# GpSimd scales all weights, ScalarE takes a small copy from VectorE, and one late layer 3 is planned shorter

## The chip, the cores and the metric

The kernel runs on one core of a Trainium2 chip. The core has five engines with a queue of instructions each, worked off in order: TensorE (PE, with its weight loads as PEld), VectorE (DVE), ScalarE (ACT), GpSimd (POOL) and SyncE (SP, which here only issues DMAs). They wait for each other through semaphores. The metric is the time of one execution on the device in microseconds (us), here the median of three.

## The reference

The input is x of shape (16, 64, 64, 256): 16 samples of 4096 tokens with 256 channels. Four layers follow each other, each of the form "x plus something computed from the group-normalized x" (`_gn`: 32 groups of 8 channels, mean and variance over a sample's tokens and a group's channels).

```python
def encode(x, embeddings):                       # layer 0
    dis = sum(xf*xf, -1) + sum(embeddings**2, 0) - 2.0 * xf @ embeddings
    return argmin(dis, -1)                       # 1024 codes
x = x + take(embeddings.T, encode(_gn(x)), axis=0)

# layer 1, rows of the 64x64 image attend within themselves
f, g, h = n @ Wf + bf, n @ Wg + bg, n @ Wh + bh  # n = _gn(x)
x = x + einsum('bhij,bhjo->bhio', sigmoid(einsum('bhik,bhjk->bhij', f, g)), h)

# layer 2, rank one attention over 4096 x 4096
x0, x1, x2 = n @ w1 + b1, n @ w2 + b2, n @ w3 + b3
sm = softmax(x0[:, :, None] * x1[:, None, :], axis=1)
x = x + sigmoid(einsum('bn,bnm->bm', x2, sm)) * n

# layer 3, linear attention with 4 heads of 32
q, k, v = split(n @ w_qkv, 3)
q = softmax(q, over the 32 channels of a head) * 32 ** -0.5
k = softmax(k, over the 4096 tokens)
out = einsum('bhde,bhdn->bhen', einsum('bhdn,bhen->bhde', k, v), q) @ w_out + b_out
x = x + layernorm(out) * gamma + beta
```

## The kernel before

**Samples in a pipeline.** Each sample goes through generators: `stats0` (statistics of x), `stage1` (layer 0, the search among 1024 codes), `layer1`, `rows2` and `stage2` (layer 2: its three rows, then its exponentials), `gate2` (layer 2's gate, and statistics for layer 3) and `stage3` (layer 3). Several samples are under way at once, each in another stage. A sample's activations go to DRAM between stages, channel-major in chunks of 512 tokens, eight chunks a sample.

**The plan.** At the end of `tile_net_kernel` (lines 938 to 974) each generator gets a start and a length in units of one search, by hand: the search of sample b starts at b and lasts 1.0; later stages follow with lags, and a stage kind never overlaps itself. A heap then steps all generators in the order of these planned times. The length says only how a generator's steps are spread among those of the others. `LEN3` (line 38) holds the length of layer 3 for the last samples, by the number of samples left (0 is the last); all others have 1.0:

```python
LEN3 = {0: 0.4, 1: 0.33, 2: 0.37}
task("layer3", end + LAG4, LEN3.get(left, 1.0), stage3(b), 160)
```

By this, layer 3 of sample 12 (the thirteenth) is planned from 15.83 to 16.83, that of sample 13 from 16.83 to 17.20, of 14 from 17.20 to 17.53, of 15 from 17.62 to 18.02. Beside sample 12's run layer 1 of sample 15 (16.06 to 16.41), its rows (16.44 to 16.54), the exponentials of sample 14 (15.93 to 16.93) and the gate of sample 13 (15.99 to 16.79).

The steps are recorded through the Tile layer, whose scheduler makes each engine's final order from this order, with what stands under `tc.high_priority(offset=URGENT)` pulled ahead, and places all semaphores. Chip and trace know only the final order of each queue.

**From statistics to weights.** `gn_finish` (lines 276 to 299) turns statistics into `scale`, `nmean` and `nbias` of 128 partitions x 2: TensorE averages over groups, ScalarE adds epsilon (line 293), GpSimd raises to the power -0.5 (line 296) and multiplies for `nbias` (line 298). The normalization isn't applied to the activations of layers 1 to 3; it is put into their weights: `scaled` (lines 301 to 308) multiplies each of two halves of a weight by that half's column of `scale`, in place, on the engine that is given:
- `layer1`, lines 459 and 460: `wfg_n` (128x64 a half) on ScalarE, `wh_n` (128x256) on VectorE. TensorE then uses them at line 464 (a bias), 163 (the row `h_row`, in `put_row`), 482 and 493 (the chunks).
- `rows2`, lines 573 to 577: `wrow_n`, 12 columns a half, on ScalarE. TensorE follows at lines 579 and 593.
- `stage3`, lines 728 and 729: `wk_n` (128x128) on ScalarE, `wqv_n` (128x256) on VectorE. TensorE follows at lines 163, 767 and 786.

Of each buffer there is one; the raw weights are loaded into it from DRAM anew for each sample by SP.

**The search.** For each chunk `norm` makes the normalized tokens and their squares on ScalarE, sums the squares on TensorE (line 357), copies the sums out of PSUM on ScalarE (`xrow`, line 362), and transposes them on TensorE into another bank (line 364). `norm_rows` (lines 366 to 369) copies four columns of that bank to `nx2` on VectorE. Per tile of 128 tokens ScalarE writes code norms plus `nx2` (line 398), TensorE multiplies (403), VectorE adds and takes the maximum (409) and finds its index (414), and GpSimd gathers the code row with an indirect DMA that adds to the tokens (415).

**The exponentials.** Each of the 64 passes of a sample takes 2048 elements per partition: ScalarE's exponential with its sum (line 645), then VectorE's product with a second SBUF tile and its sum (line 648). In layer 3 GpSimd subtracts a maximum (line 808), multiplies by a reciprocal (760) and takes a power (874).

Of the kernel before, what the change touches and what calls it, by code (L numbers as in the profile page):

```python
# [12 lines left out]
AF = mybir.ActivationFunctionType  # L13
ALU = mybir.AluOpType
AX = mybir.AxisListType

P = 128
# [17 lines left out]
LAG2 = 0.17  # L35
LAG3, LENG = 0.06, 0.8
LAG4 = 0.04
LEN3 = {0: 0.4, 1: 0.33, 2: 0.37}
FILL = ((0.05, 0.95, 2), (1.0, 1.27, 3), (1.4, 1.58, 2))
EARLY = sum(n for _, _, n in FILL)  # L40

# [2 lines left out]
def kernel(  # L44
# [7 lines left out]
    nc = tc.nc  # L52
# [17 lines left out]
    def bank(name):  # L70
        return ps_m.tile([P, 512], F32, tag="pm", name=name)
# [60 lines left out]
    def busy(t, n):  # L132

        for _ in range(n):
            nc.tensor.matmul(
                t[:, :512], lhsT=ones3, rhs=ones3.unsqueeze(1).to_broadcast([P, 4, P]), start=True, stop=True,
                skip_group_check=True,
            )
# [6 lines left out]
    def put_row(dst, v, weight, tag, plus=None, idle=0):  # L145

        v3 = small.tile([P, NK, PARTS], F32, tag="v3", name=f"v3_{tag}")
        nc.scalar.copy(v3, v.unsqueeze(2).to_broadcast([P, NK, PARTS]))
        pb = bank(f"prow_{tag}")
        busy(pb, idle)  # L150
        row = pb[:PARTS, :C]
        weight(row, v3, plus)

        for n in range(PARTS - 1):
            top = small.tile([PARTS, C], BF16, tag="ptop", name=f"top_{tag}_{n}", bufs=1)
            nc.scalar.copy(top, row)
            nc.tensor.matmul(row, lhsT=below[:, n, :], rhs=top, start=False, stop=True, skip_group_check=True)
        nc.scalar.copy(dst[0:PARTS, :], row)

    def by_weight(w):  # L160
        def make(out, v3, plus):
            for k in range(NK):
                nc.tensor.matmul(
                    out, lhsT=v3[:, k, :], rhs=w[:, k, :], start=(k == 0), stop=(plus is None and k == NK - 1),
                    skip_group_check=True,
                )
            for k in range(NK if plus is not None else 0):
                nc.tensor.matmul(
                    out[:, k * P : (k + 1) * P], lhsT=plus[:, k, :], rhs=ident, start=False, stop=(k == NK - 1),
                    skip_group_check=True,  # L170
                )
        return make
# [61 lines left out]
    wrow_raw = const.tile([P, NK, 4], F32, name="wrow_raw")  # L234
# [14 lines left out]
    for n in range(2):  # L249
        t = const.tile([P, CH, 2, ROW], F32, name=f"blk_{n}")  # L250
# [4 lines left out]
    for n in range(4):  # L255
        t = const.tile([P, 8], F32, name=f"m8_{n}")
# [44 lines left out]
    def scaled(t, scale, engine):  # L301

        for k in range(NK):
            v = t[:, k]
            if engine is nc.scalar:
                nc.scalar.activation(v, v, AF.Copy, scale=scale[:, k : k + 1])
            else:
                engine.tensor_scalar(v, v, scale[:, k : k + 1], None, ALU.mult)
# [20 lines left out]
    def stage1(b):  # L329
        tag = f"s1_{b}"  # L330
        scale, _, nbias = norm0.pop(b)
        src = xT[b].rearrange("(k p) n -> p k n", p=P)
        tok = x[b].rearrange("(t p) c -> p t c", p=P)
        xt, xc, xn, nx2, pxt = {}, {}, {}, {}, {}
# [31 lines left out]
        def norm_rows(ch):  # L366
            px = pxt.pop(ch)
            nx2[ch] = small.tile([P, CH], F32, tag="x2", name=f"nx2_{tag}_{ch}")
            nc.vector.tensor_copy(nx2[ch], px[:, :P].rearrange("p (t n) -> p t n", n=32)[:, :, 0])  # L369

        st1 = stats_tile(1, f"st1_{tag}")
        x1_d[b] = []
# [15 lines left out]
        load(1)  # L388
        norm(0)
        norm_rows(0)  # L390
        tokens(0)
        yield 4
# [48 lines left out]
    def layer1(b):  # L441
        tag = f"l1_{b}"
        scale, nmean, _ = norm1.pop(b)
        x1 = x1_d.pop(b)
        wfg_n = wts.tile([P, NK, 2 * CK], F32, tag="wfg_n", name=f"wfg_{tag}")
        load_wfg(wfg_n)
        wh_n = wts.tile([P, NK, C], F32, tag="wh_n", name=f"wh_{tag}")
# [8 lines left out]
        load(1)  # L456
        with tc.high_priority(offset=URGENT):

            scaled(wfg_n, scale, nc.scalar)
            scaled(wh_n, scale, nc.vector)  # L460
            pb = bank(f"pb_{tag}")
            for n in range(4):
                for k in range(NK):
                    nc.tensor.matmul(
                        pb[n * CK : (n + 1) * CK, 0:1], lhsT=wfg_n[:, k, (n // 2) * CK : (n // 2 + 1) * CK],
                        rhs=nmean[:, k : k + 1], start=(k == 0), stop=(k == NK - 1),
                    )
            bfg_n = small.tile([P, 1], F32, tag="bfg_n", name=f"bfg_{tag}")
            nc.scalar.activation(bfg_n, pb[:, 0:1], AF.Identity, bias=bfg)
            put_row(h_row, nmean, by_weight(wh_n), f"h_{tag}", plus=bh3)  # L470
# [96 lines left out]
    def rows2(b):  # L567
        tag = f"r2_{b}"
        scale, nmean, _ = norm2[b]
        with tc.high_priority(offset=URGENT):  # L570
            pb = bank(f"pbr_{tag}")
            busy(pb, 3)
            for k in range(NK):
                nc.scalar.activation(
                    wrow_n[:, k, :].rearrange("p (j n) -> p j n", n=32)[:, :, 0:3],
                    wrow_raw[:, k : k + 1, 0:3].to_broadcast([P, 4, 3]), AF.Copy, scale=scale[:, k : k + 1],
                )
            for k in range(NK):
                nc.tensor.matmul(
                    pb[:, 0:1], lhsT=wrow_n[:, k, :], rhs=nmean[:, k : k + 1], start=(k == 0), stop=(k == NK - 1)  # L580
                )
            brow_n = small.tile([P, 1], F32, tag="brow_n", name=f"brow_{tag}")
            nc.scalar.activation(brow_n, pb[:, 0:1], AF.Identity, bias=brow)
        x01 = small.tile([P, NT, 2], F32, tag="x01", name=f"x01_{tag}", bufs=2)
        rd = dram.tile([3, 2, 4, CW], F32, tag="rows", name=f"rows_{tag}", bufs=3)
        for h in range(2):
            pr = bank(f"pr_{tag}_{h}")
            for j in range(4):
                xt = xb.tile([P, NK, CW], F32, tag="xb", name=f"xr_{tag}_{h}_{j}")
                nc.sync.dma_start(out=xt, in_=x2_d[b][4 * h + j])  # L590
                part = slice(32 * j, 32 * j + 32)
                for k in range(NK):
                    nc.tensor.matmul(
                        pr[part, :], lhsT=wrow_n[:, k, part], rhs=xt[:, k, :], start=(k == 0), stop=(k == NK - 1)
                    )
            rows = s1p.tile([P, CW], F32, tag="t4", name=f"rows_{tag}_{h}", bufs=3)
            nc.scalar.activation(rows, pr, AF.Identity, bias=brow_n)
            for n in range(3):
                nc.scalar.dma_start(out=rd[n, h], in_=rows[n : n + 97 : 32, :])
            pt = bank(f"prt_{tag}_{h}")  # L600
            for t in range(CH):
                nc.tensor.transpose(pt[:, t * P : (t + 1) * P], rows[:, t * P : (t + 1) * P], ident)
            nc.vector.tensor_copy(
                x01[:, 16 * h : 16 * h + 16, :].rearrange("p (j t) n -> p j t n", t=CH),
                pt.rearrange("p (t j n) -> p j t n", j=4, n=32)[:, :, :, 0:2],
            )
            yield 4
        rows_d[b] = x01, rd, [spread_rows(rd, b, 0)]

    def spread_rows(rd, b, h):  # L610

        x0b = s2p.tile([P, TOK // 2], F32, tag="x0b", name=f"x0b_{b}_{h}", bufs=2)
        x2b = s2p.tile([P, TOK // 2], F32, tag="x2b", name=f"x2b_{b}_{h}", bufs=2)
        for dst, n in ((x0b, 0), (x2b, 2)):
            nc.sync.dma_start(
                out=dst, in_=rd[n : n + 1, h, :, :].rearrange("o j n -> o (j n)").to_broadcast([P, TOK // 2])
            )
        return x0b, x2b
# [98 lines left out]
    def stage3(b):  # L717
# [3 lines left out]
        scale, nmean, xm_ = norm3.pop(b)  # L721
        wk_n = wts.tile([P, NK, P], F32, tag="wk_n", name=f"wk_{tag}")
        nc.sync.dma_start(out=wk_n, in_=w_src[:, :, 1, :])
        wqv_n = wts.tile([P, NK, 2 * P], F32, tag="wqv_n", name=f"wqv_{tag}")
        nc.sync.dma_start(out=wqv_n[:, :, 0:P], in_=w_src[:, :, 0, :])
        nc.sync.dma_start(out=wqv_n[:, :, P:], in_=w_src[:, :, 2, :])
        with tc.high_priority(offset=URGENT):
            scaled(wk_n, scale, nc.scalar)
            scaled(wqv_n, scale, nc.vector)
            put_row(qv_row, nmean, by_weight(wqv_n), f"qv_{tag}")  # L730
        yield 4

# [29 lines left out]
        for ch in range(NCHUNK):  # L762
# [18 lines left out]
            for pr in range(CH // 2):  # L781
                pqv = bank(f"pqv_{tag}_{ch}_{pr}").rearrange("p (j n) -> p j n", j=2)
                for j in range(2):
                    t = 2 * pr + j
# [111 lines left out]
        for ch in range(NCHUNK):  # L896
# [4 lines left out]
            for pr in range(2):  # L901
                if pr == 1 and ch + 1 < NCHUNK:
                    deviate(ch + 1)
                px = bank(f"pxo_{tag}_{ch}_{pr}").rearrange("p (j c) -> p j c", c=C)
                for j in range(2):
                    t = 2 * pr + j
# [5 lines left out]
                for j in range(2):  # L912
                    t = 2 * pr + j
# [38 lines left out]
    for b in range(nb):  # L952
# [9 lines left out]
        else:  # L962
            end = task("exps", end + LAG2, 0.65, stage2(b, NCHUNK), 200)
        task("layer3", end + LAG4, LEN3.get(left, 1.0), stage3(b), 160)
    for _ in stats0(0):
# [3 lines left out]
    while queue:  # L969
        now, n = heapq.heappop(queue)  # L970
# [40 lines left out]
```

## Time and profile before

| | us |
|---|---|
| median of 3 executions | 5653.41 |
| lowest, highest | 5650.06, 5654.34 |
| the profiled execution | 5630.88 |
| its span, first to last instruction | 5629.1 |
| mean granted TensorE clock | 0.964 |

The costliest groups of instructions of that execution:

| line, engine | what | count | busy us | mean ns |
|---|---|---|---|---|
| 648 DVE | exponentials times x2, sum | 1024 | 2388.3 | 2340 |
| 645 ACT | exponentials, sum | 1024 | 2138.5 | 2089 |
| 403 PE | search, tokens by codes | 4096 | 1971.2 | 615 |
| 415 POOL | gather of code rows | 512 | 1140.5 | 2228 |
| 414, 409 DVE | index of the maximum, maximum | 512 each | 622.7, 620.1 | 1217, 1213 |
| 398 ACT | code norms plus token norm | 512 | 583.3 | 1145 |
| 808, 760 POOL | layer 3, subtract, multiply | 128 each | 249.7, 198.0 | 1951, 1547 |

How to read it: "busy" is the time an engine works on such instructions. A row of a group also has the idle time of the engine just before these instructions and what ended it, so it names what an engine waited for; the view of waits lists the same by pair. A window of the trace gives busy times for a stretch alone. Matmuls are pipelined and their ends modelled, so a busy TensorE need not be at its peak.

### The profile page before, as it was taken

To read this page: it belongs to the slowest core of one execution; us is meant where nothing else is said; L and a number is where in the kernel's file an instruction comes from. 1 tells how busy PE (TensorE), PEld (TensorE's weight loads), DVE (VectorE), ACT (ScalarE), POOL (GpSimd) and SP (SyncE) were. 2 spreads that over 40 slices of the span, in tenths; PEclk is the share of its full clock that TensorE was granted. 3 is DMA by queue.
4 is the path that set the end of the run, shared out by engine and by line. 5 is a ranking of instruction groups with operands and counts; after the bars stand their busy time and mean duration, and the time that the engine had idled before them with its cause. 6 is when DMAs were issued, how large, how long until landed. Compare 5 with 4: busy or idle time off the path is not lost. (4 is left out here: it accounts for less than half of the span.)

```text
span 5629.1 us, 76169 instructions
## 1 busy us (share of the span) xinstructions
PE 5138.9 (91%) x26927; PEld 3174.3 (56%) x26927; DVE 5068.5 (90%) x7186; ACT 4560.2 (81%) x6642; POOL 1832.7 (33%) x1076
## 2 busy tenths in 40 slices
PE   7977989989999999999999999999999999997788
PEld 3533446545656556565655656565565656665566
DVE  7579789899999999999999999999999999988982
ACT  4468589788879888887988888798888979888873
POOL 2223223323333333433333343333334334321231
PEclk9988999999999999999999999999999999998889
DMA  8552744755665757566575756757575675745643
GB/s 253 173 184 73 227 132 123 226 166 174 192 214 150 235 156 228 184 204 221 164 251 152 230 175 207 228 155 247 154 226 183 204 226 152 231 152 193 203 158 121
DMA packets 521366, 1059.26 MB, mean 188 GB/s; under 512 B 52505, under 2 KB 266393, under 8 KB 512793
## 3 DMA queue, kind: packets, MB, share of 16 engines
q1 hardware_dynamic: 406288, 885.11, 46.9%
q0 software_dynamic: 73728, 67.14, 8.5%
q10 hardware_dynamic: 40968, 102.13, 4.7%
q8 instruction: 214, 3.51, 0.3%
q14 instruction: 168, 1.37, 0.1%
HBM read 751.18 MB, written 303.04 MB: 187 GB/s over the span
## 5 line engine op out<-in xcount | busy, mean ns | idle before, releaser
L648 DVE CUSTOM_DVE_ANT_0 ex_s<-ex_s,x2b 128x2048 f32<-128x2048 f32 x1024 | 2388.3, 2340 | 55.7 <-ACT ex_s L645 54.2
L645 ACT ACTIVATE ex_s<-x0b,nmax_s,x_r 128x2048 f32<-128x2048 f32 x1024 | 2138.5, 2089 | 40.3 <-DVE num_s L648 28.8
L403 PE MATMUL pd_s<-e,xn_s 128*128 128x512 f32 x4096 | 1971.2, 615 | 54.0 <-DVE m L409 41.8
L415 POOL DMA_INDIRECT xc_s<-in_emb_rows,i_s x512 | 1140.5, 2228 | 1778.4 <-DVE i_s L414 1274.6
L403 PEld LDWEIGHTS pd_s<-e,xn_s 128*128 128x128 f32 x4096 | 747.3, 196 | 786.9 <-issue 666.4
L409 DVE CUSTOM_DVE_ANT_0 nn_s<-pd_s,nn_s 128x1024 f32<-128x1024 f32 x512 | 620.1, 1213 | 114.4 <-PE pd_s L403 72.3
L414 DVE FIND_INDEX8 i_s<-m,nn_s 128x8 uint32<-128x1024 f32 x512 | 622.7, 1217 | 0.0
L398 ACT ACTIVATE nn_s<-ne,nx_s 128x1024 f32<-128x1024 f32 x512 | 583.3, 1145 | 40.7 <-DVE nx_s L369 24.8
L493 PE MATMUL ph_l<-wh_l,xt_l 128*128 128x256 f32 x2048 | 522.2, 392 | 33.8 <-DVE m L409 27.5
L786 PE MATMUL pqv_s<-wqv_s,xk_s 128*128 128x256 f32 x2048 | 489.3, 381 | 0.0
L493 PEld LDWEIGHTS ph_l<-wh_l,xt_l 128*128 128x128 f32 x2048 | 383.2, 194 | 144.9 <-issue 72.7
L786 PEld LDWEIGHTS pqv_s<-wqv_s,xk_s 128*128 128x128 f32 x2048 | 389.4, 191 | 120.7 <-issue 60.8
L808 POOL TENSOR_TENSOR qv_s<-qv_s,qm_s 128x512 f32<-128x512 f32 x128 | 249.7, 1951 | 580.6 <-DVE qm_s L807 316.0
L874 POOL TENSOR_TENSOR lrs_s<-lrs_s,mhalf 128x4 f32<-128x4 f32 x128 | 172.3, 1346 | 662.7 <-ACT lrs_s L873 655.3
L760 POOL TENSOR_TENSOR qv_s<-qv_s,qd_s 128x512 f32<-128x512 f32 x128 | 198.0, 1547 | 378.2 <-DVE qd_s L759 249.5
L378 PE MATMUL pt_s<-ident,xc_s 128*128 128x128 f32 x1024 | 163.0, 288 | 127.6 <-DMA xc_s<-in_emb_rows,i_s 102.3
L533 PE MATMUL po_l<-blk,h_l 128*128 128x128 f32 x2048 | 272.5, 282 | 3.2 <-DVE m L409 3.2
L533 PEld LDWEIGHTS po_l<-blk,h_l 128*128 128x128 f32 x2048 | 251.2, 194 | 36.8 <-issue 19.9
L914 PE MATMUL pxo_s<-wctx_s,qo_s 128*128 128x256 f32 x1024 | 267.8, 385 | 0.0
L767 PE MATMUL pk_s<-xk_s,wk_s 128*128 128x512 f32 x512 | 252.5, 616 | 1.4 <-DMA xk_s<-x_g 1.4
L378 PEld LDWEIGHTS pt_s<-ident,xc_s 128*128 128x128 f32 x1024 | 123.2, 147 | 191.7 <-DMA xc_s<-in_emb_rows,i_s 120.4
L919 ACT COPY y_s<-pxo_s 128x512 f32<-128x512 f32 x256 | 147.6, 580 | 103.2 <-PE pxo_s L918 102.4
(206 smaller groups left out, 7372.6 us busy)
## 6 DMA issues: line engine op xcount, KB each, us to landing
xs_s<-in_xT SPq DMA_DIRECT2D x128, 512.0 KB
xt_s<-in_xT SPq DMA_DIRECT2D x128, 512.0 KB
xc_s<-in_x SPq DMA_DIRECT2D x128, 512.0 KB
x_s<-xt_s ACTq DMA_DIRECT2D x128, 512.0 KB
xt_l<-x_s SPq DMA_DIRECT2D x128, 512.0 KB
x_l<-xt_l SPq DMA_DIRECT2D x128, 512.0 KB
xr_r<-x_l SPq DMA_DIRECT2D x128, 512.0 KB
xg_g<-x_l SPq DMA_DIRECT2D x128, 512.0 KB
```

Of the source, the lines that this page charges most:

```text
L378: nc.tensor.transpose(pt[:, t * P : (t + 1) * P], xc[ch][:, t, k * P : (k + 1) * P], ident)
L398: nc.scalar.activation(nn, ne2, AF.Identity, bias=nx2[ch][:, t : t + 1])
L403: nc.tensor.matmul(pd[:, cols], lhsT=xn[ch][:, k, t * P : (t + 1) * P], rhs=e2[:, k, cols], start=(k == 0), stop=(k == NK - 1),)
L409: nc.vector.tensor_tensor_reduce(out=nn, in0=pd, in1=nn, scale=1.0, scalar=-3.0e38, op0=ALU.add, op1=ALU.max, accum_out=m8[:, 0:1],)
L414: nc.vector.max_index(i8, m8, nn)
L415: nc.gpsimd.indirect_dma_start(out=xc[ch][:, t, :], out_offset=None, in_=emb_rows, in_offset=bass.IndirectOffsetOnAxis(ap=i8[:, 0:1], axis=0),
L493: nc.tensor.matmul(ph[:, t, :], lhsT=X[:, k, t * P : (t + 1) * P], rhs=wh_n[:, k, :], start=(t % 2 == 0 and k == 0), stop=False, skip_grou ...
L533: nc.tensor.matmul(po[:, m : m + P], lhsT=h[:, t, k * P : (k + 1) * P], rhs=at[:, t, :, :].rearrange("p r i -> p (r i)"), start=True, stop ...
L645: nc.scalar.activation(ex, x0b, AF.Exp, bias=nmax[:, T : T + 1], scale=x01[:, T, 1:2], accum_out=den[:, h, T : T + 1])
L648: nc.vector.tensor_tensor_reduce(out=ex, in0=ex, in1=x2b, scale=1.0, scalar=0.0, op0=ALU.mult, op1=ALU.add, accum_out=num[:, h, T : T + 1],)
L786: nc.tensor.matmul(pqv[:, j, :], lhsT=xt[:, k, t * P : (t + 1) * P], rhs=wqv_n[:, k, :], start=(j == 0 and k == 0), stop=False, skip_group ...
L914: nc.tensor.matmul(px[:, j, :], lhsT=qT[:, t * P : (t + 1) * P], rhs=wctx[:, 1, :], start=False, stop=False, skip_group_check=True,)
```

## The change

Three edits. All five weights are now scaled on GpSimd, two instructions each. VectorE's copy of the token norms becomes one of ScalarE. Layer 3 of sample 12 (three samples left) gets the length 0.7, so that it is planned from 15.83 to 16.53; the starts and lengths of all other stages stay as they were.

```diff
-LEN3 = {0: 0.4, 1: 0.33, 2: 0.37}
+LEN3 = {0: 0.4, 1: 0.33, 2: 0.37, 3: 0.7}
...
-            nc.vector.tensor_copy(nx2[ch], px[:, :P].rearrange("p (t n) -> p t n", n=32)[:, :, 0])
+            nc.scalar.copy(nx2[ch], px[:, :P].rearrange("p (t n) -> p t n", n=32)[:, :, 0])
...
-            scaled(wfg_n, scale, nc.scalar)
-            scaled(wh_n, scale, nc.vector)
+            scaled(wfg_n, scale, nc.gpsimd)
+            scaled(wh_n, scale, nc.gpsimd)
...
-                nc.scalar.activation(
+                nc.gpsimd.tensor_scalar(
                     wrow_n[:, k, :].rearrange("p (j n) -> p j n", n=32)[:, :, 0:3],
-                    wrow_raw[:, k : k + 1, 0:3].to_broadcast([P, 4, 3]), AF.Copy, scale=scale[:, k : k + 1],
+                    wrow_raw[:, k : k + 1, 0:3].to_broadcast([P, 4, 3]), scale[:, k : k + 1], None, ALU.mult,
                 )
...
-            scaled(wk_n, scale, nc.scalar)
-            scaled(wqv_n, scale, nc.vector)
+            scaled(wk_n, scale, nc.gpsimd)
+            scaled(wqv_n, scale, nc.gpsimd)
```

## The prediction

> **What bounds the kernel now.** I read the engine totals first, then the chain of waits, then busy time by stage, then DVE's waits inside the steady stage, and last the rows of the edited instructions. Totals and chain:
>
> ```profile
> PE 5138.9 (91%) x26927; PEld 3174.3 (56%) x26927; DVE 5068.5 (90%) x7186; ACT 4560.2 (81%) x6642; POOL 1832.7 (33%) x1076
> ...
> PE 5%; ACT 3%; DVE 2%; DMA 1%; issue 0%; POOL 0%; ACTq 0%; SPq 0%; POOLq 0%
> ```
>
> The chain's shares add up to about 12%: it reaches back only to 4958 us, where the last search ends, so it tells of the tail alone. For the rest I cut the span by stage. GpSimd's line 629 comes once a sample: at 1309 us for sample 3, at 4924 for sample 14, and between them every 322 to 334 us. These are eleven steady periods of about 329 us (columns: window, length, busy us and count of PE, PEld, DVE, ACT, POOL, then clock, DMA share, GB/s):
>
> ```profile
> 0.00:700.00 700.00, 574.90 (x2614) 300.20 (x2614) 540.02 (x832) 412.37 (x573) 187.10 (x138) 0.91 0.60 181
> ...
> 1309.00:4924.00 3615.00, 3431.22 (x18456) 2136.80 (x18455) 3437.54 (x4838) 3115.41 (x4542) 1295.65 (x720) 0.99 0.63 198
> 4924.00:5200.00 276.00, 231.20 (x1328) 160.70 (x1327) 244.94 (x321) 233.81 (x352) 56.55 (x39) 0.91 0.52 174
> 5200.00:5490.00 290.00, 231.30 (x1105) 166.83 (x1103) 251.54 (x367) 228.27 (x352) 76.17 (x49) 0.88 0.54 179
> ```
>
> In the steady stage DVE is 95.1% busy, PE 94.9%, ACT 86%, POOL 36%: two engines are full together, and neither alone bounds. DVE idles 177 us there (3615 less 3437.54); its waits in that window say on what:
>
> ```profile
> DVE ex_s L648 <- ACT ex_s L645: 38.3, 37, 2.7
> DVE wh_l L308 <- POOL gn_s_n L296: 29.0, 11, 2.6
> DVE nkm_s L770 <- PE pk_s L767: 26.3, 18, 3.4
> ...
> DVE wqv_s L308 <- POOL gn_s_n L296: 10.8, 11, 1.7
> ```
>
> The second and fourth are the edited lines: 22 times DVE reaches a weight before GpSimd has raised the scale to its power, and holds its queue.
>
> **DVE's relief.** The edited rows over the whole run, DVE's and the ones that leave ACT:
>
> ```profile
> L306 ACT ACTIVATE wk_s<-wk_s,gn_s_n 128x128 f32<-128x128 f32 x32 | 11.0, 391 | 4.3 <-POOL gn_s_n L296 4.3
> L308 DVE TENSOR_SCALAR wqv_s<-wqv_s,gn_s_n 128x256 f32<-128x256 f32 x32 | 10.4, 364 | 16.5 <-POOL gn_s_n L296 16.5
> L308 DVE TENSOR_SCALAR wh_l<-wh_l,gn_s_n 128x256 f32<-128x256 f32 x32 | 10.4, 363 | 34.0 <-POOL gn_s_n L296 34.0
> L306 ACT ACTIVATE wfg_l<-wfg_l,gn_s_n 128x64 f32<-128x64 f32 x32 | 9.4, 340 | 27.0 <-POOL gn_s_n L296 27.0
> L574 ACT ACTIVATE wrow_n<-wrow_raw,gn_s_n 128x12 f32<-128x12 f32 x32 | 8.1, 296 | 19.8 <-POOL gn_s_n L296 19.6
> L369 DVE COPY nx_s<-pxt_s 128x4 f32<-128x4 f32 x128 | 19.4, 151 | 23.3 <-PE pxt_s L364 23.3
> ```
>
> In eleven periods DVE loses 44 scalings x 0.325 us (10.4/32) = 14.3, 88 norm copies x 0.151 = 13.3, and waits of 29.0 + 10.8 = 39.8: together 67 us, 6.1 a period. The copies' own 23.3 us of waiting lies almost wholly before 700 us, where DVE isn't full; I count none of it.
>
> **ACT.** It loses 11.0 + 9.4 + 8.1 = 28.5 us of scaling and 27.0 + 4.3 + 19.6 = 50.9 of waiting. It gains 128 copies; bounds are 0.19 us (line 148's 128x6 copy) and 0.26 (line 362's 128x128 copy out of PSUM), so 24 to 33 us. Its busy time stays. Could the copy wait? In the steady stage the transpose at line 364 ends 0.38 to 1.81 us after ACT's copy at line 362. In the built order 107 of the 128 new copies have a pass of line 645 (2.09 + 0.19 us) or 398 (1.15) in between, so I cost the wait at nothing. Were that cover gone it would be 88 x 0.81 us (the mean) = 71 us on ACT, which idles 500 us there. Line 398, which waited 24.8 us for DVE's copy, now follows on the same engine.
>
> **GpSimd.** No tensor-by-scalar operation of POOL is in the trace. Nearest rows (least, median, greatest ns):
>
> ```profile
> L298 POOL TENSOR_TENSOR gn_nb_n<-gn_nm_n,gn_s_n x48: 186/188/1841, 193.2 to 5501.9; 128x2 f32<-128x2 f32 x48
> L760 POOL TENSOR_TENSOR qv_s<-qv_s,qd_s x128: 1042/1290/3195, 859.3 to 5575.6; 128x512 f32<-128x512 f32 x128
> L808 POOL TENSOR_TENSOR qv_s<-qv_s,qm_s x128: 1038/1654/3142, 844.5 to 5572.0; 128x512 f32<-128x512 f32 x128
> ```
>
> Between 186 ns for 2 elements and 1038 for 512 lie 1.67 ns an element. My estimates: 0.20 us for wrow (12), 0.29 for wfg (64), 0.40 for wk (128), 0.61 for wh and wqv (256); above, 1.65 each (line 808's median), below, 0.19. Ten a sample take 4.2 us; POOL idles 210 us a period.
>
> All now follow line 298 (0.19 us) in one queue. wh is ready 0.19 + 0.58 + 1.22 = 2.0 us after the power, against 0.69 now; wqv 0.19 + 0.80 + 1.22 = 2.2 against 0.69. Who waits? From the end of a scaling to PE's first use the steady stage has at least 1.4 us for wfg, 4.8 for wh, 20 for wk and wqv: nothing. In samples 0 to 2 the slack of wh is 0.12 to 0.17, so PE starts 1.2 us late three times: 3.5. Sample 15's wqv has 0.27 and sample 13's 0.85: 1.3 + 0.7. wrow has none (PE starts the moment it ends): 0.19 + 0.40 against 0.53 now, 0.1 x 15 = 1.5. Sum +7; at 1.65 us an operation some +75, at 0.19 each +1. Behind them on POOL stand the gathers of line 415 and lines 808, 760, 874; ACT waits for 808 (51.4 us in 22 waits in the steady stage), so up to 2 us at one of those now and then.
>
> The row that speaks against the change: of the 1024 passes of line 648, the 750 that meet no GpSimd tensor operation average 2.28 us; 79 that meet one of line 808, 2.43; 55 with line 760, 2.88; 17 with both, 3.28; 84 with the power of line 874, 2.28. So a 1.04 us GpSimd operation costs DVE 0.15 to 0.60 us, a tiny one nothing. Ten of 0.42 us on average: 0.6 to 2.4 us a period; I take 1.0, so 11 of the 67 go back and 56 stay.
> The Trainium skill (SBUF — State Buffer, "Who interferes with whom") goes further: a VectorE instruction with two SBUF inputs, as line 648 is, and a GpSimd instruction that reads SBUF lock each other out, the later one for the whole of the earlier. By that, an estimate, 42% (2388/5629) of 4.2 us, 1.8 a period, goes back, and the forecast would be 4 us later.
>
> **Layer 3 of sample 12.** It starts at planned time 15.83 and is spread to 16.53, not 16.83; layer 3 of sample 13 keeps 16.83. Its fetches (line 764, 898, 823), stores and POOL steps move with it. In DVE's order its last step stands after pass 935 of line 648 instead of 948, the first maximum of sample 13 after 945 instead of 956; from 972 on both orders agree within two passes, so the last 139 us are untouched. From 4924 to 5490 us DVE idles 70 us, which bounds any gain; 18.8 of it lies in 5066 to 5207, where the step moves. Sample 15's rows fall 2 to 4 passes (4.2 us each) later, with over 60 us left until its first pass at 5197. I take -6; bounds -20 and +15.
>
> **The sum.** PE and DVE tie, so I let half of 56 come through: -28, +7, -6 = -27. The profiled execution has a span of 5629.1 us, 5630.9 with what lies around it; the median shown is 22.5 higher, and I carry the difference over: 5653.4 - 27 = 5626.
>
> **Rivals.**
> - DVE is the true bound and all 56 come through: -56 + 7 - 6, 5598. For: DVE's waits for PE are some 58 us of the 177. Against: PE idles only 184 us.
> - PE takes over at once: +7 - 6, 5654. For: PE's 94.9%. Against: PE itself waits for DVE's line 409 (24.4 + 16.5 us) there.
> - Slower: the scalings collide with line 648. All ten a period meet a pass and lengthen it by 1.0 us (the row that meets two): 10 - 6.1 = 3.9 lost a period, 43, half of it 22 with the +1: 5676. It decides from 0.61 us an operation, line 760's row. For: line 648 fills 42% of the span. Against: most weight operations are far smaller, and the power costs passes nothing.
> - The tail turns: sample 15's rows come over 60 us late, or the denser layer 3 stalls the passes: -28 + 7 + 40, 5672. Against: its order hardly moves.
>
> **How the numbers follow.** Half relief 0.46, full relief 0.22, PE takes over 0.12, collision 0.13, tail 0.07. A median of this kernel can be told from no change at about 0.2%, 11 us: 5642 to 5665. Half relief (own range 5605 to 5646) is faster in nine cases of ten: faster 0.41 + 0.22 + some 0.04 from the third = 0.67; same 0.05 + 0.07 = 0.12; slower 0.21. The range runs from full relief with the tail's -20 (5584, some 5 lower for relief before 1309 us) to just short of the collision: 5580 to 5672.
>
> **What would show it.** Right: the period at line 629 falls from 329 us to about 326; DVE has no waits for POOL's scale; line 648's mean stays under 2.40 us (2.34 now); PE's idle time in the steady stage shrinks below 184 us. Wrong: line 308 on POOL takes over 1 us each, or line 648 passes 2.45; PE waits for POOL at line 163 or 464 in the steady stage; the period stays while DVE's idle time grows; or the stretch after 4924 us, 705 now, changes by over 15.

## The result, and the profile after

The changed kernel takes 5691.03 us (median of 6 runs, 5683.00 to 5704.59), the kernel before on the same chip 5653.07 (6 runs, 5636.73 to 5659.93): a ratio of 1.0077, 95% interval [1.0062, 1.0091]. The change makes the kernel slower by some 38 us of median; 5626 with a range of 5580 to 5672 had been predicted. The sign was wrong, and the time lies outside the range.

The profiled execution of the changed kernel has a span of 5691.2 us. Its totals, and the group of line 648:

```profile
PE 5175.6 (91%) x26927; PEld 3187.5 (56%) x26927; DVE 5023.9 (88%) x6994; ACT 4549.4 (80%) x6674; POOL 2033.8 (36%) x1236
...
L648 DVE CUSTOM_DVE_ANT_0 ex_s<-ex_s,x2b 128x2048 f32<-128x2048 f32 x1024 | 2361.4, 2314 | 89.1 <-ACT ex_s L645 88.8
```

VectorE did get its relief: 44.6 us less busy time (5068.5 before), and the passes of line 648 became no longer (2314 ns, before 2340). VectorE loses it again as waiting: it idles 667 us of the span, 561 before. TensorE's busy time is 36.7 us longer for as many matmuls (5138.9 before), at a granted clock of 0.958 against 0.964, so these two executions differ in the clock too. The six runs of the changed kernel had 0.957 to 0.960, and 29 runs of the kernel before on another chip 0.958 to 0.964. Whether PE's waits lower the clock isn't shown.

The same steady window as before (length; busy us and count of PE, PEld, DVE, ACT, POOL; clock, DMA share, GB/s):

```profile
1309.00:4924.00 3615.00, 3430.99 (x18303) 2131.99 (x18302) 3365.05 (x4663) 3082.75 (x4527) 1413.19 (x815) 0.98 0.63 195
```

PE is busy as before (3431), but has done 153 fewer matmuls in it, and DVE idles 250 us where it idled 177. Not all of that is the change's: in the profiled execution of s_len below, whose queues differ from those of the kernel before only from 4915 us on (but for a swap of two PE instructions), the window holds 100 fewer matmuls, and DVE idles 200 us. The runs below decide on the causes; the views show where to look. The view of waits of the whole run (waiting engine, tile and line, what ended the wait; us in total, times, longest) names the places:

```profile
DVE nn_s L409 <- PE pd_s L403: 148.0, 86, 11.4
...
DVE ex_s L648 <- ACT ex_s L645: 88.8, 78, 7.0
...
ACT brow_r L583 <- PE pbr_r L579: 51.1, 15, 4.8
...
PE pbr_r L579 <- POOL wrow_n L574: 37.1, 23, 3.0
```

The same view of the kernel before, where ScalarE scales `wrow_n`, has

```profile
PE pbr_r L579 <- ACT wrow_n L574: 16.1, 10, 1.7
...
ACT brow_r L583 <- PE pbr_r L579: 8.8, 12, 2.8
```

and 72.3 and 54.2 us for the first two pairs. VectorE no longer waits for the scale, but for PE and ACT, and these stand around lines 579 and 583, behind GpSimd's `wrow_n`. DVE's waits for the scale (29.0 + 10.8 us before) are gone, as planned.

The new operations, one row for each weight (count: ns least/median/greatest, first and last start):

```profile
L308 POOL TENSOR_SCALAR wfg_l<-wfg_l,gn_s_n x32: 432/449/2572, 197.5 to 5036.1; 128x64 f32<-128x64 f32 x32
L308 POOL TENSOR_SCALAR wh_l<-wh_l,gn_s_n x32: 912/917/5096, 198.3 to 5041.6; 128x256 f32<-128x256 f32 x32
L308 POOL TENSOR_SCALAR wk_s<-wk_s,gn_s_n x32: 592/606/2680, 805.0 to 5565.5; 128x128 f32<-128x128 f32 x32
L308 POOL TENSOR_SCALAR wqv_s<-wqv_s,gn_s_n x32: 912/915/2995, 806.2 to 5566.9; 128x256 f32<-128x256 f32 x32
...
L574 POOL TENSOR_SCALAR wrow_n<-wrow_raw,gn_s_n x32: 306/321/2423, 301.8 to 5178.7; 128x12 f32<-128x12 f32 x32
```

Least and median agree, so each operation has a time of its own (0.31, 0.45, 0.60, 0.91 us), and some take up to seven times that. Taken from the trace one by one, 121 of the 160 take their own time. The other 39 take 2.27 to 5.10 us, and every one of these began while a pass of line 648 ran on VectorE, or at most 0.05 us before it. They end 0.17 to 0.78 us after a pass ends. Operations beside other VectorE instructions (lines 266, 409, 414, 770 and more) keep their own time.

### The profile page after: what moved, and what is told of

Same layout as the page of the kernel before. It is cut to its first block, busy times and chain, and to the rows that moved or that the text cites. A ratio compares the mean times of both kernels' runs of the same rounds, so it can differ in the third digit from the quotient of the medians.

```text
span 5691.2 us, 76111 instructions
## 1 busy us (share of the span) xinstructions
PE 5175.6 (91%) x26927; PEld 3187.5 (56%) x26927; DVE 5023.9 (88%) x6994; ACT 4549.4 (80%) x6674; POOL 2033.8 (36%) x1236
## 5 line engine op out<-in xcount | busy, mean ns | idle before, releaser
L648 DVE CUSTOM_DVE_ANT_0 ex_s<-ex_s,x2b 128x2048 f32<-128x2048 f32 x1024 | 2361.4, 2314 | 89.1 <-ACT ex_s L645 88.8
L403 PE MATMUL pd_s<-e,xn_s 128*128 128x512 f32 x4096 | 2000.4, 622 | 34.3 <-DVE m L409 23.0
L415 POOL DMA_INDIRECT xc_s<-in_emb_rows,i_s x512 | 1124.7, 2197 | 1729.3 <-DVE i_s L414 1330.7
L403 PEld LDWEIGHTS pd_s<-e,xn_s 128*128 128x128 f32 x4096 | 758.7, 198 | 783.5 <-issue 697.5
L808 POOL TENSOR_TENSOR qv_s<-qv_s,qm_s 128x512 f32<-128x512 f32 x128 | 233.3, 1823 | 566.5 <-DVE qm_s L807 326.3
L874 POOL TENSOR_TENSOR lrs_s<-lrs_s,mhalf 128x4 f32<-128x4 f32 x128 | 214.5, 1676 | 572.1 <-ACT lrs_s L873 541.0
L760 POOL TENSOR_TENSOR qv_s<-qv_s,qd_s 128x512 f32<-128x512 f32 x128 | 178.2, 1392 | 369.9 <-DVE qd_s L759 157.1
L348 ACT ACTIVATE xn_s<-xt_s,first 128x512 f32<-128x512 f32 x256 | 202.2, 806 | 35.8 <-DMA xt_s<-in_xT 30.1
```

Source lines behind the costliest of these rows:

```text
L403: nc.tensor.matmul(pd[:, cols], lhsT=xn[ch][:, k, t * P : (t + 1) * P], rhs=e2[:, k, cols], start=(k == 0), stop=(k == NK - 1),)
L415: nc.gpsimd.indirect_dma_start(out=xc[ch][:, t, :], out_offset=None, in_=emb_rows, in_offset=bass.IndirectOffsetOnAxis(ap=i8[:, 0:1], axis=0),
L648: nc.vector.tensor_tensor_reduce(out=ex, in0=ex, in1=x2b, scale=1.0, scalar=0.0, op0=ALU.mult, op1=ALU.add, accum_out=num[:, h, T : T + 1],)
```

## The experiments

All ratios are to runs of the kernel before on the same chip, with 95% intervals.

### The change taken apart

Four runs each make one part of the change in the kernel before.

s_row, only `wrow` on GpSimd:

```diff
-                nc.scalar.activation(
+                nc.gpsimd.tensor_scalar(
...
-                    wrow_raw[:, k : k + 1, 0:3].to_broadcast([P, 4, 3]), AF.Copy, scale=scale[:, k : k + 1],
+                    wrow_raw[:, k : k + 1, 0:3].to_broadcast([P, 4, 3]), scale[:, k : k + 1], None, ALU.mult,
```

> Only rows2's small weight wrow is scaled on GpSimd, all else as before. Theory A (the scaling on GpSimd comes late, because a GpSimd operation that reads SBUF stands behind VectorE's exponential pass, and TensorE waits for the weight at the head of its queue): slower, +10 to +25 us, and TensorE's waits for wrow at line 579 rise from 16 to over 30 us. Theory B (the norm copy on ScalarE is what costs): no change, within 8 us. Theory C (the shorter layer 3 of sample 12 costs at the end): no change, within 8 us.

s_w4, only the other four weights on GpSimd:

```diff
-            scaled(wfg_n, scale, nc.scalar)
-            scaled(wh_n, scale, nc.vector)
+            scaled(wfg_n, scale, nc.gpsimd)
+            scaled(wh_n, scale, nc.gpsimd)
...
-            scaled(wk_n, scale, nc.scalar)
-            scaled(wqv_n, scale, nc.vector)
+            scaled(wk_n, scale, nc.gpsimd)
+            scaled(wqv_n, scale, nc.gpsimd)
```

> Only the four weights of line 308 (wfg, wh, wk, wqv) are scaled on GpSimd, wrow as before. Theory A: slower by +5 to +20 us, with new waits of TensorE at lines 163 and 464 of some 25 us, most of them in the first three samples and the last two. Theories B and C: not slower, rather 5 to 20 us faster, since VectorE loses 71 us of scaling and waiting for the scale.

s_nx, only the copy of the norms on ScalarE:

```diff
-            nc.vector.tensor_copy(nx2[ch], px[:, :P].rearrange("p (t n) -> p t n", n=32)[:, :, 0])
+            nc.scalar.copy(nx2[ch], px[:, :P].rearrange("p (t n) -> p t n", n=32)[:, :, 0])
```

> Only the copy of the token norms moves to ScalarE. Theory A: no change or faster, -15 to +5 us, since VectorE loses 19 us of copies and ScalarE finds a pass to do before the transpose is ready. Theory B: slower by 20 us or more, with the passes of line 648 waiting longer for ScalarE. Theory C: as A.

s_len, only the planner's entry:

```diff
-LEN3 = {0: 0.4, 1: 0.33, 2: 0.37}
+LEN3 = {0: 0.4, 1: 0.33, 2: 0.37, 3: 0.7}
```

> Only the length 0.7 for layer 3 of sample 12. Theories A and B: -10 to +8 us, and nothing different before 4600 us. Theory C: slower by 10 us or more, all of it after 4900 us.

Measured, all four against 5647.51 us:

| run | part | median us | ratio |
|---|---|---|---|
| s_row | `wrow` on GpSimd | 5682.41 | 1.0076 [1.0058, 1.0095] |
| s_w4 | four weights on GpSimd | 5647.02 | 1.0005 [0.9993, 1.0017] |
| s_nx | copy on ScalarE | 5632.37 | 0.9977 [0.9964, 0.9991] |
| s_len | layer 3 of sample 12 | 5648.24 | 1.0004 [0.9991, 1.0018] |

The smallest part, 32 operations on 12 columns, holds the whole loss. The copy is a gain of 0.23%; the four large weights, taken together over all samples, and the planner's entry change nothing that can be measured. Theory A had the direction of s_row and PE's waits at line 579 (44.4 us), but 10 to 25 us in place of 35. The interval of s_w4, -4 to +10 us, leaves out the 5 to 20 us faster of theories B and C. The four add up to 1.0062, a little under the 1.0077 of the whole, whose interval begins there.

What `wrow` does is seen at sample 9 in the order of time (start us, us, engine, line and operation; in brackets the idle time before and what ended it). The kernel before:

```profile
3244.39 1.21 DVE L414 FIND_INDEX8 i_s<-m,nn_s 128x8 uint32<-128x1024 f32 x1
3244.41 0.72 POOL L296 TENSOR_TENSOR gn_s_n<-gn_s_n,mhalf 128x2 f32<-128x2 f32 x1
3245.16 0.50 ACT L574 ACTIVATE wrow_n<-wrow_raw,gn_s_n 128x12 f32<-128x12 f32 x2 [2.04 <-POOL gn_s_n L296]
...
3245.52 0.61 PE L579 MATMUL pbr_r<-gn_nm_n,wrow_n 128*128 128x1 f32 x4 [1.73 <-ACT wrow_n L574]
3245.53 2.27 DVE L648 CUSTOM_DVE_ANT_0 ex_s<-ex_s,x2b 128x2048 f32<-128x2048 f32 x1
...
3246.17 0.26 ACT L583 ACTIVATE brow_r<-pbr_r,brow 128x1 f32<-128x1 f32 x1 [0.50 <-PE pbr_r L579]
```

s_row at the same place:

```profile
3266.00 0.72 POOL L296 TENSOR_TENSOR gn_s_n<-gn_s_n,mhalf 128x2 f32<-128x2 f32 x1
3266.81 0.18 POOL L298 TENSOR_TENSOR gn_nb_n<-gn_nm_n,gn_s_n 128x2 f32<-128x2 f32 x1
3266.98 2.58 POOL L574 TENSOR_SCALAR wrow_n<-wrow_raw,gn_s_n 128x12 f32<-128x12 f32 x2
3267.12 2.27 DVE L648 CUSTOM_DVE_ANT_0 ex_s<-ex_s,x2b 128x2048 f32<-128x2048 f32 x1
...
3267.35 0.38 PE L579 MATMUL pbr_r<-gn_nm_n,wrow_n 128*128 128x1 f32 x2 [1.97 <-POOL wrow_n L574]
...
3269.62 0.59 PE L579 MATMUL pbr_r<-gn_nm_n,wrow_n 128*128 128x1 f32 x2 [1.88 <-POOL wrow_n L574]
...
3270.24 0.26 ACT L583 ACTIVATE brow_r<-pbr_r,brow 128x1 f32<-128x1 f32 x1 [5.52 <-PE pbr_r L579]
```

Before, `wrow` is done 0.53 us after the power. VectorE's pass has begun 0.13 us earlier, and ScalarE isn't held up by it. In s_row the product of line 298 comes first, then the first half of `wrow` (0.32 us). While that runs VectorE begins its next pass; the second half stands until the pass is over and takes 2.27 us in place of 0.31. PE has done two of its four matmuls of line 579 and stands another 1.88 us at the head of its queue; ACT, whose next instruction is line 583, stands 5.52 us (before 2.04 + 0.50); so VectorE's next exponentials come late too, and it idles. In samples 7 to 13 every turn looks like this, `wrow` within a few ns: 316 ns and 2267 ns. In samples 3, 6, 14 and 15 the second half stands as well, in 4 and 5 the product of line 298 does. In samples 0 to 2, where no pass runs at that time, the halves take 326 and 313 ns.

The size fits as well: PE's waits at line 579 are 16.1 us over the run before, and in s_row

```profile
ACT brow_r L583 <- PE pbr_r L579: 60.7, 15, 5.5
...
PE pbr_r L579 <- POOL wrow_n L574: 44.4, 23, 3.4
```

which is 28 us more for PE; 35 us were lost (5682.41 less 5647.51).

### Is it the second operation?

If the second operation stands because it comes too late for the gap between two VectorE passes, one operation for both halves must take most of the loss away, with `wrow` still on GpSimd. In e_oneop the scale is broadcast; the order of all other instructions on every engine is that of s_row.

```diff
-            for k in range(NK):
-                nc.gpsimd.tensor_scalar(
-                    wrow_n[:, k, :].rearrange("p (j n) -> p j n", n=32)[:, :, 0:3],
-                    wrow_raw[:, k : k + 1, 0:3].to_broadcast([P, 4, 3]), scale[:, k : k + 1], None, ALU.mult,
-                )
+            nc.gpsimd.tensor_tensor(
+                wrow_n.rearrange("p k (j n) -> p k j n", n=32)[:, :, :, 0:3],
+                wrow_raw[:, :, 0:3].unsqueeze(2).to_broadcast([P, NK, 4, 3]),
+                scale.unsqueeze(2).unsqueeze(3).to_broadcast([P, NK, 4, 3]), ALU.mult,
+            )
```

> As s_row, but GpSimd scales wrow with one instruction in place of two (both halves in one product with the scale broadcast). Theory A1 (the loss is the second of two short GpSimd operations, which finds VectorE's next pass begun and stands behind it): the one instruction follows the power at once, takes under 0.6 us in the steady stage, TensorE's wait at line 579 there falls from 3.85 to about 2.0 us, and the time is within 10 us of before. Theory A2 (any scaling on GpSimd after the power is late, for the way between the engines or for what else stands in its queue): still +20 us or more.

Measured: 5655.21 us, 1.0024 [1.0011, 1.0037], against 5642.6: 13 us over the kernel before, a little more than the 10 that theory A1 allowed, and less than A2's 20. The same sample:

```profile
3282.07 0.19 POOL L298 TENSOR_TENSOR gn_nb_n<-gn_nm_n,gn_s_n 128x2 f32<-128x2 f32 x1
3282.22 0.22 POOL L573 TENSOR_TENSOR wrow_n<-wrow_raw,gn_s_n 128x24 f32<-128x24 f32 x1
3282.38 2.27 DVE L648 CUSTOM_DVE_ANT_0 ex_s<-ex_s,x2b 128x2048 f32<-128x2048 f32 x1
...
3282.49 0.61 PE L579 MATMUL pbr_r<-gn_nm_n,wrow_n 128*128 128x1 f32 x4 [1.84 <-POOL wrow_n L573]
```

The operation has begun 0.16 us before the pass does, and takes its own 0.22 us; PE's gap is back at 1.84 us (1.73 before). It removes 0.52 of the 0.76%, some 29 us; PE's waits at line 579 over the run fall by 20 us, from 44.4 to 24.2. So most of the cost isn't that GpSimd does the work, but that it starts after VectorE's pass has begun.

e_nonb tries the other way to the same end: two operations, but the product of line 298 ahead of them left out where its result isn't read (all norms but the first, `n0`).

```diff
-        nbias = held(2, "gn_nb", kind, b)
-        nc.gpsimd.tensor_tensor(nbias, nmean, scale, ALU.mult)
+        nbias = None
+        if kind == "n0":
+            nbias = held(2, "gn_nb", kind, b)
+            nc.gpsimd.tensor_tensor(nbias, nmean, scale, ALU.mult)
```

> As s_row, two instructions on GpSimd, but the product for nbias that stands between the power and the scaling (0.19 us) is left out where it isn't used (the norms of layers 1 to 3). Theory A1: the second scaling now begins 0.19 us earlier, about 1.14 us after VectorE's last pass ended, before the next pass begins at some 1.3; it takes 0.3 us in place of 2.27, and the loss goes: within 10 us of before. Theory A2: 0.19 us a sample earlier is worth 3 us at most, so still +35 us or more.

Measured: 5694.47 us, 1.0094 [1.0079, 1.011]: no gain over s_row. That is the number of A2, but the trace shows the lock again. The pass begins 0.39 us after the power has ended, as in s_row (0.40), since VectorE is free by then and waits for nothing of this. That is 1.13 us after the last pass's end; the expectation had it at 1.3. Without the product the first half runs from 0.11 to 0.43 us after the power, so the second still comes after the pass's begin, by 0.03 us, and stands: 2.42 us in samples 7 to 13. Being late by a little costs as much as being late by more.

### The rest of the change

p_norow is the whole change, with `wrow` left on ScalarE.

```diff
-                nc.gpsimd.tensor_scalar(
+                nc.scalar.activation(
...
-                    wrow_raw[:, k : k + 1, 0:3].to_broadcast([P, 4, 3]), scale[:, k : k + 1], None, ALU.mult,
+                    wrow_raw[:, k : k + 1, 0:3].to_broadcast([P, 4, 3]), AF.Copy, scale=scale[:, k : k + 1],
```

> The whole change except wrow, which stays on ScalarE. Theory A: the norm copy's gain is left, 5625 to 5650 us, ratio 0.996 to 1.001; steady period 327 to 328.5 us. If the parts don't add up (another theory: the order of all queues as a whole): over 5665 us.

Measured: 5640.34 us, 0.9999 [0.9985, 1.0012]. Without the 32 operations on `wrow` the loss is gone. But the gain of the copy (0.9977) isn't left over either; something in the other parts seems to eat it. Its waits show where to look. Before 1300 us, where samples 0 to 2 run with little beside them:

```profile
PE pb_l L464 <- POOL wfg_l L308: 11.9, 6, 5.0
```

The kernel before waited 3.8 us there for ScalarE's `wfg`. In samples 1 and 2 the first half of `wfg` takes 2.50 us on GpSimd: it stands behind a pass too. And after 4920 us, with the last samples, in the same view:

```profile
PE prow_qv_s L163 <- POOL wqv_s L308: 10.4, 2, 7.0
...
PE ph_l L493 <- POOL wh_l L308: 2.4, 1, 2.4
```

So b_best1 takes GpSimd for the four weights only where other work stands ready, keeps the copy on ScalarE and `wrow` on ScalarE, and leaves the planner's entry out (the lines that replace those of the kernel before, but for the copy's):

```diff
+            scaled(wfg_n, scale, nc.gpsimd if 2 < b < nb - 1 else nc.scalar)
+            scaled(wh_n, scale, nc.gpsimd if 2 < b < nb - 1 else nc.vector)
...
+            scaled(wk_n, scale, nc.gpsimd if b < nb - 3 else nc.scalar)
+            scaled(wqv_n, scale, nc.gpsimd if b < nb - 3 else nc.vector)
```

> A version meant to beat both: the norm copy on ScalarE, wrow on ScalarE, the four weights on GpSimd only in the steady stage (layer 1 of samples 3 to 14, layer 3 of samples 0 to 12) where TensorE has microseconds of slack, lengths as before. Theory A: 5615 to 5635 us, ratio 0.994 to 0.998. If the gains of the norm copy and the four weights are the same time counted twice: as s_nx, 0.9975 to 0.9985.

Measured: 5627.90 us, 0.9975 [0.9961, 0.9989]. That is the copy's gain, and no more: beside the copy, the four weights on GpSimd bring nothing in the steady stage. b_best1 differs from p_norow in two things, so b_best1len adds the planner's entry to it:

```diff
-LEN3 = {0: 0.4, 1: 0.33, 2: 0.37}
+LEN3 = {0: 0.4, 1: 0.33, 2: 0.37, 3: 0.7}
```

> b_best1 with the one planner entry of the change added: layer 3 of sample 12 in seven tenths of a period. Theory (the entry does nothing by itself, as s_len showed): 0.9965 to 0.9990, as b_best1 has 0.9975. Rival (p_norow lost the gain of b_best1 through this entry, not through GpSimd scaling in the first three and last three samples): 0.9985 to 1.0010.

Measured: 5624.05 us, 0.9973 [0.9958, 0.9988], against 5641.39. The entry is harmless here too. b_best1len differs from p_norow only in who scales in the first and last samples, so what p_norow lost, 0.26% or some 15 us, comes with GpSimd scaling there. b_best1len is the fastest kernel of the study and beats both, though s_nx, which changes one line, can't be told from it.

### The lock in the whole change

a_oneop is the whole change with one operation for `wrow`, edited as in e_oneop; all other instructions keep the changed kernel's order.

> The whole change, with wrow scaled by one GpSimd operation in place of two; on every engine the order of the rest is that of the changed kernel. Theory (the second of the two operations stands behind VectorE's 2.28 us pass, and PE behind it at line 579): between s_row and e_oneop this was worth 0.52%, and the same 0.4 to 0.6% comes back here, so the ratio falls from 1.0077 to about 1.0025, with PE's wait at line 579 near 1.85 us in samples 7 to 13 instead of 3.85. Rival (in the whole change the four other weights crowd the same queue, so that the one operation stands behind them or behind a pass as well): the ratio stays at 1.006 or more.

Measured: 5651.11 us, 1.0013 [0.9997, 1.0029], against 5641.39. One edit of 32 instructions into 16 takes 0.64% off the changed kernel (1.0077 less 1.0013), so the cause found in s_row is the cause of the loss in the whole change as well. PE's waits at line 579, 37.1 us in the changed kernel, are in a_oneop

```profile
PE pbr_r L579 <- POOL wrow_n L573: 15.9, 13, 2.8
```

as many as the 16.1 us of the kernel before. Two numbers of the expectation were off. A little more came back than 0.4 to 0.6%, and in samples 7 to 13 PE's gap there is 1.11 us, not 1.85, since in this order the power itself is done 0.7 us sooner after line 293 (1.27 us, against 2.00 in e_oneop).

e_onenb goes back to e_oneop and leaves out the unused product of line 298, as e_nonb did, to see whether that is the 0.24% which e_oneop still lost.

> Only wrow on GpSimd, as one operation, and the product of line 298 (nbias) left out where nothing reads it, in all norms but the first. Theory: what e_oneop still lost (ratio 1.0024) is partly the product ahead of wrow in GpSimd's queue, which in samples 4 and 5 stands behind a pass (wrow ends 2.1 us after the power there, 0.46 elsewhere); without it wrow itself begins 0.1 us after the power and ends before the pass begins, and the ratio falls to 0.999 to 1.0015. Rival (the loss left is the instruction order, or wrow itself meets the pass in those two samples): it stays at 1.002 or more, and wrow takes about 2 us in samples 4 and 5.

Measured: 5649.54 us, 1.0015 [1.0000, 1.0030]. The ratio lies at the upper end of the theory's range, and its interval takes in the rival's 1.002 as well, so it doesn't decide. The durations are the rival's: in samples 4 and 5 `wrow` itself now stands, 1.85 us, in a pass that has begun before it, and PE's gap there is 3.07 us where the product had made it 3.25. In all other samples `wrow` ends 0.31 us after the power, sooner than ScalarE did (0.53). Over the run PE waits 22.1 us at its matmuls for `wrow` (e_oneop 24.2, before 16.1), and these two samples hold about all of the 6 that are more than before. What the product of line 298 is worth stays open: the two intervals overlap, and a few instructions of PE, ScalarE and VectorE stand in another order than in the kernel before.

## Why the prediction was wrong

**The step that failed: the price of `wrow`.** The prediction saw that PE starts the moment `wrow` ends, and priced its move as "0.19 + 0.40 against 0.53 now, 0.1 x 15 = 1.5". Measured alone it costs 35 us (s_row). With -13 us for the copy and some +15 for the weights at both ends (below), these make 37 of the 38 measured; -27 had been forecast. Its own time was under-estimated, 0.31 us an operation and not 0.20. What mattered is that the second half takes 2.27 us. The 188 ns of line 298 was the median of a row whose greatest value was 1841, printed in the prediction itself. The trace of before held the answer: of line 688, an operation on two columns like line 298's, the row reads

```profile
L688 POOL TENSOR_TENSOR xm_g<-bet,gn_nm_n x16: 192/1648/2270, 294.5 to 5177.6; 128x2 f32<-128x2 f32 x16
```

192 ns of its own, and in 14 of 16 cases a pass of line 648 ran at its begin: 2.02 us in the median of these. Line 808 splits the same way: 1.05 us in the 67 that begin outside a pass, 3.06 in the 61 that begin within one. Split by what VectorE does when they begin, the POOL rows of before would have shown two times for each operation.

**The lock was read in one direction.** The prediction priced what a GpSimd operation does to the passes ("a tiny one nothing") and never what a pass does to the GpSimd operation. The Trainium skill (SBUF — State Buffer, "Who interferes with whom") says that the later of the two is blocked for the whole of the earlier. The runs agree for the case that counts here, where GpSimd is the later: 2.27 us in place of 0.31. For the other the mean says nothing (in the changed kernel some 40 passes that begin while a weight operation runs average 2.29 us, those that meet none 2.31), but the passes one by one do. A pass that begins very soon after a weight operation is longer, by as much as it comes too soon:

| operation (run) | the pass begins after it, us | the pass takes, us | sum, us |
|---|---|---|---|
| `wh` (s_w4) | 0.083 | 2.529 | 2.612 |
| `wqv` (s_w4) | 0.120 | 2.492 | 2.612 |
| `wh` (s_w4) | 0.174 | 2.437 | 2.611 |
| `wh` (b_best1len) | 0.245 | 2.366 | 2.611 |
| `wqv` (after) | 0.357 | 2.280 | 2.637 |
| `wk` (after) | 0.082 | 2.423 | 2.505 |
| `wfg` (after) | 0.110 | 2.335 | 2.445 |
| `wrow` (after) | 0.065 | 2.340 | 2.405 |

With a pass of 2.28 us alone, `wh` and `wqv` hold it back until 0.33 us after their begin, `wk` until 0.23, `wfg` 0.17, `wrow` 0.13, though they run up to 0.91 us. So where GpSimd is the earlier, it blocks not for the whole of its recorded time, but for its first part. A pass that begins later than that, as at the place shown of s_row (0.13 us after the first half of `wrow`), loses nothing. In the changed kernel all this adds up to 0.3 us. So the 11 us which the prediction gave back for lengthened passes weren't lost, and the slower rival, "the scalings collide with line 648", had the right pair and the wrong victim; its point of decision, 0.61 us an operation, doesn't apply. Its 5676 us came nearest to the measured 5691 by another way. The victim is PE's queue.

**VectorE's relief from the weights.** 14.3 us of scalings and 39.8 us of waits over the eleven periods were counted, half of it to come through. Beside the copy none did: b_best1, without the ends, is at the copy's own gain. In s_w4's steady window DVE's waits for the scale are gone, and others have grown in their place; this one wasn't in the view before:

```profile
DVE ctx_s L813 <- PE pc_s L811: 22.7, 18, 3.1
```

The waits for lines 645 and 753 went from 38.3 to 43.0 and from 10.5 to 17.4 us. DVE idles 180 us of the window, as it did (177). What the weights bring alone stays open. s_w4, at 1.0005, carries both ends too, which cost 0.26% beside the copy, so its steady stage may have gained as much. In its profiled execution the time between line 629 of sample 3 and that of sample 14 falls from 3615 to 3601 us, and that from there to the end grows from 705 to 727, but s_len, with the steady stage unchanged, took 3643 in its own. A run of b_best1's weights without the copy is missing. That PE and DVE tie had been seen, and "PE takes over at once" stood among the rivals, at 0.12; the step that failed is the half.

**The copy.** 13.3 us of relief were counted, at nothing for ScalarE, and 0.23% (13 us, interval 5 to 20) came. That the two numbers agree is luck as far as the runs show, since VectorE was relieved of more: its busy time falls from 5068.5 to 5031.6 us in s_nx, where the passes of line 648 became shorter as well.

```profile
L648 DVE CUSTOM_DVE_ANT_0 ex_s<-ex_s,x2b 128x2048 f32<-128x2048 f32 x1024 | 2359.2, 2311 | 62.8 <-ACT ex_s L645 62.3
```

Before, their mean was 2340 ns: 151 of them met a GpSimd operation of lines 760 or 808, and 127 do in s_nx. So a third of the relief came through. ScalarE's copy takes 162 ns in the median, a little under the lower bound of 0.19, and waits 12.5 us for line 364 in the whole run of s_nx, so its cover held.

**The weights at both ends.** +7 us were forecast, some 15 measured (p_norow against b_best1len). The step missing is `wfg`: it was given slack "in the steady stage" and no price in samples 0 to 2, where PE waits 11.9 us for it, in samples 1 and 2 because it stands behind a pass. `wqv` at the end was named, at 2.0 us, against the 10.4 above; `wh` at the end (2.4) wasn't, and `wh` in samples 0 to 2 was priced at 3.5 and cost 1.4.

**Layer 3 of sample 12.** -6 us forecast, between -20 and +15; nothing measured (1.0004, and 0.9973 beside 0.9975).

**What should have shown it.** Of the signs listed ahead, "line 308 on POOL takes over 1 us each" came true (1.18 us in the mean: 151.0 us over 128), and so did that DVE's idle time grows, and that PE waits for POOL at lines 163 and 464 in the steady stage (10.8 us for `wh` and 4.4 for `wfg` in the window from 1309 to 4924 us, where the prediction had found slack enough). The period did not stay but rose, from 329.2 to 332.4 us between samples 4 and 14, from one line 583 to the next in the two profiled executions. Single executions differ by up to 0.7% among themselves, and s_len, with the same steady stage as before, had 331.5, so the ratios show the size. Two signs of being right came true as well, no waits for the scale and a mean of line 648 under 2.40 us, and told nothing of the time. A sign at line 579 wasn't on the list; that was the place.

## What to carry to other kernels

Price an operation on GpSimd twice: once when VectorE is free, once when it begins inside VectorE's longest instruction with two SBUF inputs, and take the second where an engine stands for the result. The distribution of GpSimd's durations, least and greatest beside the median, tells whether this occurs; a mean hides it. What feeds the head of another engine's queue within a microsecond is best left on an engine that such a pass doesn't stop (ScalarE's halves of `wrow` took 0.29 to 0.30 us in samples 4 and 5 of the kernel before, where they began inside a pass), or done in a single operation that begins before the pass.

And relief of one engine need not come through where another is as full. Here 36.9 us less work of a 95% busy VectorE were worth 13, and 14 us of scalings with 40 us of waits besides were worth nothing more. That the 95% busy PE is the reason is argued, not tested.

## What had not been expected of the hardware

One GpSimd operation on 24 elements a partition with a broadcast operand (tensor by tensor) takes 0.22 us, less than one on 12 elements with a scalar column (0.31 us). The time of the latter kind grows as 0.31, 0.45, 0.60, 0.91 us for 12, 64, 128, 256 elements, about 2.5 ns an element from 64 on.

Whether a GpSimd operation stands is decided at about its begin. In the changed kernel operations that began 0.051 us or less ahead of a pass's begin stood for all of it (31, 45, 46, 46 and 51 ns ahead: 2.54 to 2.57 us), and those that began 0.065 us or more ahead ran through beside it in their own time (65, 82 and 110 ns ahead: 0.32, 0.61, 0.45 us), and the pass was the longer one (2.34, 2.42, 2.34 us). The first five are all `wfg`, the others of different weights. In s_w4, p_norow, a_oneop and b_best1len nothing speaks against a border there: up to 48 ns ahead all stood, from 83 ns on all ran through. One `wh` operation stood for a second pass as well and took 5.10 us in place of 0.91.
